# Layer 1 (windowed attention) of a four-layer megakernel, redone: centred weights, paired value products, norm copies on POOL, softmax in parts, source order on four engines

## The chip, the cores and the metric

The kernel runs on one core of one Trainium2 chip. The metric is the device time of one launch in microseconds (us), as the median of the runs shown. Everything is float32.

## The reference

Four residual layers are applied to an image batch x of 8 x 56 x 56 x 192 (NHWC). Each is `x = x + layer(group_norm(x))`, with a group norm of 32 groups of 6 channels. The layers are a Toeplitz token mixer, a shifted-window attention, a depthwise convolution with four exponential scans, and a 7x7 depthwise convolution with an MLP. The change touches the second, which is cut here to what matters:

```python
mu = jnp.mean(x, axis=-1, keepdims=True)              # over the 192 channels
var = jnp.var(x, axis=-1, keepdims=True)
x = (x - mu) * jax.lax.rsqrt(var + EPS) * gamma + beta
sx = jnp.roll(x, shift=(-3, -3), axis=(1, 2))
win = <7x7 windows of sx>                              # 64 windows of 49 tokens per image
q, k, v = (win @ w_qkv + b_qkv)                        # 6 heads of 32
attn = softmax(q * hd**-0.5 @ k.T + rel_bias + mask)
out = (attn @ v) @ w_proj + b_proj                     # windows back to the image, roll back
```

## The kernel before, in words

The launch runs layer 0, layer 1, layer 2 and layer 3 one after the other, each over all 8 images, with the images in DRAM between them. Channels lie on partitions: 64 channels of three blocks j = 0, 1, 2, and the upper and the lower half of an image on partitions 0 to 63 and 64 to 127 (s = 0, 1).

Layer 1 works on one image in four groups g. A group is one row of eight 7x7 windows in each half, so 392 tokens (TT) per half. A group's work is cut into parts, each a Python closure that issues its instructions when it is called:

- **N**: one step of the generator `layer1_norm` for the next image. It copies the image with the group norm's scale and shift into window order in `xr` (L703, five ACT activations per group), gets the mean over channels with a matmul of ones (L707) and subtracts it on DVE (L709), squares on ACT (L711), gets the variance with a second matmul (L715), and, once per image, takes root and reciprocal (L727, L728) and multiplies (L689, L691).
- **Q** (four per group): `project` in `layer1_scores`, matmuls of q or k for 96 of 192 channels (L748) and their evictions on ACT and DVE (L754 to L758).
- **V** (two per group): `values`, for each window and each half of the channels a product with 64 tokens as the stationary operand and 96 columns of weights as the moving one (L767), evicted on ACT and DVE (L775, L777).
- **E** (two per group, one per half s): `weights`. 48 small products of q and k into the PSUM tile S (L788), then bias and mask added on DVE (L795), the maximum (L797), its subtraction on POOL (L798), exp on ACT (L799), the sum and its reciprocal on DVE (L801, L802), and the multiplication on POOL (L803).
- **T** (six per group): `turn`, four transposes of the attention weights on PE (L823) into the `et_ps` tile, and a copy on ACT or DVE.
- **P** (two): `mix`, 48 small products of the weights with v (L838), and two copies that put windows back into image rows (L849, L851).
- **R** (three): `project` in `layer1_mix`, the output projection (L857) and its addition to the image on DVE (L864).

PSUM has three banks under the tag `mm`, taken in turn by Q, V, P, R and the norm (two each for Q, V and P), two for the transposes and three for S. While a group is mixed (T, P, R), the next one is projected and scored (Q, V, E), and the next image is normed (N), in an order that is written out by hand and holds for PE alone; what the other engines do, and when, is ordered by the planner from its own costs:

```python
plan = "T T Q N T T Q T P N T Q N Q P E N V E N V R R R".split()
st.enter_context(tc.manual_schedule(engines={mybir.EngineType.PE}))
```

The SP queue loads the images (`layer1_load`, three buffers), loads bias and mask for each half group (`bm`, two buffers) and stores the results. `build_bias_mask` prepares bias and mask during layer 0. The bn_stats for the group norm of layer 2 (L154) follow each group.

Of the kernel before, what the change touches and what calls it, by code (L numbers as in the profile page):

```python
# [10 lines left out]
F32 = mybir.dt.float32  # L11
# [8 lines left out]
HC = 96  # L20
TT = 392
# [8 lines left out]
HEADS, HD, WN = 6, 32, 49  # L30

# [56 lines left out]
def kernel(ctx: ExitStack, tc: tile.TileContext, a: dict, out: bass.AP):  # L88
# [215 lines left out]
    def build_bias_mask(psum, pool, masks):  # L304
# [31 lines left out]
        def add(g):  # L336
            bm = pool.tile([128, 3, 4, 2, WN], F32, name="bmt", bufs=1)
            for h in range(HEADS):
                nc.vector.tensor_tensor(
                    bm[:, h % 3, :, h // 3, :], mks[g], bt[:, h:h + 1, :].to_broadcast([128, 4, WN]), ALU.add  # L340
                )
            nc.gpsimd.dma_start(bmask[g], bm.rearrange("p a b c d -> p (a b c d)"))
# [277 lines left out]
    def layer1_weights(pool, psum):  # L620
# [29 lines left out]
        wg = pool.tile([128, 3, 3 * C], F32, name="wg", bufs=1)  # L650
        for j in range(3):
            nc.vector.tensor_scalar(wg[:, j], w_qkv[:, j], vec("g1", j), None, ALU.mult)
        nc.vector.tensor_scalar(wg[:, :, 0:C], wg[:, :, 0:C], HD ** -0.5, None, ALU.mult)
        return wg, bq, w_proj, bpr
# [19 lines left out]

    def layer1_norm(b, x, pool, psum, consts, first=False):

        ones2, ones32, sel = consts[4:]

        xr = pool.tile([128, 3 * NH + 16], F32, name="xr")
        nc.gpsimd.memset(xr[:, 3 * NH:], 0.0)
        xw = xr[:, 0:3 * NH].rearrange("p (j n) -> p j n", j=3)
        rs = pool.tile([128, TT], F32, name="rs1")

        def scaled(g):
            gs = bass.ts(g, TT)
            bp = psum.tile([128, 512], F32, name="rstd", tag="mm", bufs=3)[:, 0:TT]
            nc.tensor.matmul(bp, sel[32 * g:32 * g + 32], rs[32 * g:32 * g + 32], start=True, stop=True)  # L689
            xs = xw[:, :, gs]  # L690
            nc.vector.tensor_tensor(xs, xs, bp.unsqueeze(1).to_broadcast([128, 3, TT]), ALU.mult)  # L691

        yield xr
        sc, sh = scsh1[:, 0, b:b + 1], scsh1[:, 1, b:b + 1]
        for g in range(4):
            gs = bass.ts(g, TT)
            windows = xw[:, :, gs].rearrange("p c (w i j) -> p c w i j", i=7, j=7)
            xg = x[:, :, 7 * g:7 * g + 7]
            for dst, src in (
                *((windows[:, j, 0:7], xg[:, j, :, 3:52].rearrange("p i (w j) -> p w i j", j=7)) for j in range(3)),  # L700
                (windows[:, :, 7, :, 0:4], xg[:, :, :, 52:56]), (windows[:, :, 7, :, 4:7], xg[:, :, :, 0:3]),
            ):
                nc.scalar.activation(dst, src, AF.Identity, bias=sh, scale=sc)  # L703
            yield
            mp = psum.tile([128, 512], F32, name="mean", tag="mm", bufs=3)[:, 0:TT]
            for j in range(3):
                nc.tensor.matmul(mp, ones2, xw[:, j, gs], start=(j == 0), stop=(j == 2))  # L707
            xs = xw[:, :, gs]
            nc.vector.tensor_tensor(xs, xs, mp.unsqueeze(1).to_broadcast([128, 3, TT]), ALU.subtract)  # L709
            sq = pool.tile([128, 3, TT], F32, name="sq")  # L710
            nc.scalar.activation(sq, xs, AF.Square)  # L711
            yield
            vp = psum.tile([128, 512], F32, name="vps", tag="mm", bufs=3)[32 * g:32 * g + 32, 0:TT]
            for j in range(3):
                nc.tensor.matmul(vp, ones32, sq[:, j], start=(j == 0), stop=(j == 2))  # L715
            if not first:
                nc.vector.tensor_copy(rs[32 * g:32 * g + 32], vp)
                continue
            rg = rs[32 * g:32 * g + 32]
            nc.scalar.activation(rg, vp, AF.Sqrt, bias=eps5[32 * g:32 * g + 32])  # L720
            nc.vector.reciprocal(rg, rg)
            yield
            scaled(g)
            yield
        if first:
            return
        nc.scalar.activation(rs, rs, AF.Sqrt, bias=eps5)  # L727
        nc.vector.reciprocal(rs, rs)  # L728
        for g in range(4):
            yield  # L730
            scaled(g)

    def layer1_scores(g, xr, pool, psum, S, es, consts):
# [3 lines left out]
        xw = xr[:, 0:3 * NH].rearrange("p (j n) -> p j n", j=3)  # L737
        gs = bass.ts(g, TT)
        qk = [pool.tile([HC, 2, 2, TT], F32, name=f"qk{s}", bufs=1) for s in range(2)]

        v = [pool.tile([128, 8, HC], F32, name=f"v{s}") for s in range(2)]

        def project(which, m):
            ps = [psum.tile([128, 512], F32, name="qk_ps", tag="mm", bufs=3)[0:HC, 0:TT] for s in range(2)]
            c0 = which * C + m * HC
            for j in range(3):
                for s in range(2):
                    nc.tensor.matmul(  # L748
                        ps[s], wg[64 * s:64 * s + 64, j, c0:c0 + HC], xw[64 * s:64 * s + 64, j, gs],
                        start=(j == 0), stop=(j == 2),  # L750
                    )
# [8 lines left out]
        def values(w4):  # L760
            ps = [psum.tile([128, 512], F32, name="v_ps", tag="mm", bufs=3)[:, 0:4 * HC] for s in range(2)]
            for w in range(4):
                for j in range(3):
                    for p in range(2):
                        for s in range(2):
                            t0 = j * NH + g * TT + WN * (w4 + w)
                            nc.tensor.matmul(  # L767
                                ps[s][64 * p:64 * p + 64, HC * w:HC * w + HC], xr[64 * s:64 * s + 64, t0:t0 + 64],
                                wg[64 * s:64 * s + 64, j, 2 * C + HC * p:2 * C + HC * p + HC],
                                start=(j == 0), stop=(j == 2),  # L770
                            )
            for s in range(2):
                dst = v[s][:, w4:w4 + 4].rearrange("p w c -> p (w c)")
# [5 lines left out]
        def weights(s):  # L779
            bm = pool.tile([128, 24, WN], F32, name="bm")  # L780
            nc.sync.dma_start(bm.rearrange("p a b -> p (a b)"), bmask[4 * s + g])


            for w in range(8):
                cs = slice(WN * w, WN * w + WN)
                for h in range(HEADS):
                    p0 = 32 * (h % 3)
                    nc.tensor.matmul(  # L788
                        S[64 * (w % 2):64 * (w % 2) + WN, 8 * (h % 3) + w // 2 * 2 + h // 3, 0:WN],
                        qk[s][p0:p0 + 32, 0, h // 3, cs], qk[s][p0:p0 + 32, 1, h // 3, cs],  # L790
                        start=True, stop=True,
                    )
            e = es[g % 2][s]
            ev = e[:, :, 0:WN]
# [3 lines left out]
            nc.gpsimd.tensor_tensor(ev, ev, mx.unsqueeze(2).to_broadcast([128, 24, WN]), ALU.subtract)  # L798
            nc.scalar.activation(ev, ev, AF.Exp)  # L799
            sm = pool.tile([128, 24], F32, name="sm")  # L800
# [4 lines left out]
        return v, [  # L805
            [lambda which=which, m=m: project(which, m) for which in range(2) for m in range(2)],
            [lambda w4=w4: values(w4) for w4 in (0, 4)], [lambda s=s: weights(s) for s in range(2)],
        ]

    def layer1_mix(g, x, v, pool, psum, es, consts):  # L810
# [21 lines left out]
        def mix(s):  # L832
            et, o = ets[s], oa[s]
            po = [psum.tile([128, 512], F32, name="po", tag="mm", bufs=3)[0:HC, 0:TT] for _ in range(2)]
            for w in range(8):
                for r in range(3):
                    for hh in range(2):
                        nc.tensor.matmul(  # L838
                            po[hh][32 * r:32 * r + 32, WN * w:WN * w + WN],
                            v[s][64 * hh:64 * hh + WN, w, HD * r:HD * r + HD],  # L840
                            et[64 * hh:64 * hh + WN, 4 * r + w // 2, 64 * (w % 2):64 * (w % 2) + WN],
                            start=True, stop=True,
                        )

            for hh in range(2):
                dst = o[:, hh].rearrange("p (i w j) -> p w i j", i=7, j=7)
                src = po[hh].rearrange("p (w i j) -> p w i j", i=7, j=7)
                if hh == 0:
# [4 lines left out]
        def project(j):  # L853
            ps = psum.tile([128, 512], F32, name="pr", tag="mm", bufs=3)[:, 0:TT]
            for m in range(2):
                for s in range(2):
                    nc.tensor.matmul(  # L857
                        ps[64 * s:64 * s + 64], w_proj[:, m, 64 * j:64 * j + 64], oa[s][:, m],
                        start=(m == 0), stop=(m == 1),
# [6 lines left out]
        return [  # L866
            [lambda s=s, i=i: turn(s, i) for s in range(2) for i in range(3)],
            [lambda s=s: mix(s) for s in range(2)], [lambda j=j: project(j) for j in range(3)],
        ]
# [447 lines left out]
    with ExitStack() as st:  # L1317
        pool = st.enter_context(tc.tile_pool(reuse_waits="tile", name="l1", bufs=2))
        psum = st.enter_context(tc.tile_pool(reuse_waits="tile", name="l1p", bufs=1, space=PSUM))
        consts = layer1_weights(pool, psum)  # L1320

# [5 lines left out]
        for s in range(2):  # L1327
            nc.gpsimd.memset(ones2[64 * s:64 * s + 64, 64 * s:64 * s + 64], 1.0 / C)
            nc.gpsimd.memset(ones32[64 * s:64 * s + 64, 16 * s:16 * s + 16], 1.0 / C)
        nc.gpsimd.dma_start(sel, a["sel"])  # L1330
# [6 lines left out]
        consts = (*consts, ones2, ones32, sel)  # L1337
# [3 lines left out]
        for _ in range(4):  # L1341
            next(own)
        if nimg > 1:
            x.append(layer1_load(1, xpool))
        values, (Q, V, E) = layer1_scores(0, xr[0], pool, psum, S, es, consts)
# [263 lines left out]
```

## Time and profile before

| what | value |
|---|---|
| median of three runs | 5983.35 us (5983.24 to 5999.2) |
| the profiled execution | 5980.23 us |
| its span | 5978.3 us |
| busy share of PE, DVE, ACT, POOL over the span | 89%, 56%, 37%, 22% |
| layer 1, from the last store of layer 0 to the last addition (L864) | 2055.7 to 3366.3 us |
| busy in images 1 to 6 of it (952.5 us): PE, DVE, ACT, POOL | 805.33, 493.99, 328.67, 209.77 us |
| granted TensorE clock there | 0.92 |

The span runs from the first to the last instruction of the profiled execution; the launch's own time is 1.9 us longer. Busy time is the union of an engine's instructions, and PE's is modelled, since matmuls are pipelined. A float32 matmul shows up as two PE instructions (passes), each with its weight load (PEld). A wait named "issue" is time in which an engine waited for nothing that the profile shows.

### The profile page before, as it was taken

The numbers are of one execution on the slowest core, as the hardware profiler recorded it, in microseconds if no ns is written. First come the engines' busy times: TensorE is split into PE (matmuls) and PEld (weight loads), VectorE is DVE, ScalarE is ACT, GpSimd is POOL, SyncE is SP. The second block draws the span as 40 slices with busy tenths as digits, with TensorE's granted clock in tenths as the row PEclk, the third lists the DMA queues.
The fourth block names the chain that finished last, engine by engine and source line by source line (L and its number), as shares of the span: only waits on it lengthen the run. The fifth ranks groups of instructions, "written<-read, shape, count | busy, mean of one in ns | idle before, by whom it ended". The sixth has DMA issues, their size and how long they took to land. (4 is left out here: it accounts for less than half of the span.)

```text
span 5978.3 us, 124904 instructions
## 1 busy us (share of the span) xinstructions
PE 5305.3 (89%) x54932; PEld 3442.4 (58%) x54932; DVE 3367.4 (56%) x4698; ACT 2225.5 (37%) x2993; POOL 1299.5 (22%) x862
## 2 busy tenths in 40 slices
PE   6899989999998888888888798999788799799999
PEld 4668756666665545455555475777444399444444
DVE  6777765555555455554555586888877401533331
ACT  2344443333333333333332102455466600333333
POOL 2100024444444212222222102333201100200100
PEclk8999989999999999899998899999899899899999
DMA  6899886666666502222211576677577598321210
GB/s 176 208 229 219 193 249 246 242 259 255 256 252 252 156 26 67 67 66 59 67 51 55 136 256 224 229 233 235 162 214 209 181 337 292 126 76 59 90 41 25
DMA packets 703411, 1012.59 MB, mean 169 GB/s; under 512 B 484888, under 2 KB 621636, under 8 KB 676100
## 3 DMA queue, kind: packets, MB, share of 16 engines
q1 hardware_dynamic: 688464, 940.25, 50.4%
q0 software_dynamic: 8256, 39.67, 2.0%
q10 hardware_dynamic: 6148, 24.68, 1.3%
q8 instruction: 432, 7.08, 0.5%
q14 instruction: 111, 0.91, 0.0%
HBM read 675.89 MB, written 345.08 MB: 171 GB/s over the span
## 5 line engine op out<-in xcount | busy, mean ns | idle before, releaser
L383 PE MATMUL qv<-w_qv_sb,xn 64*112 64x288 f32 x5376 | 710.0, 420 | 41.5 <-DVE act L389 38.0
L421 POOL COPY lc<-lt 128x896 f32<-128x896 f32 (+1 forms) x320 | 550.5, 1744 | 646.2 <-PE op L429 544.0
L383 PEld LDWEIGHTS qv<-w_qv_sb,xn 64*112 64x112 f32 x5376 | 535.5, 181 | 211.0 <-DVE act L389 53.9
L390 ACT ACTIVATE act<-act 112x576 f32<-112x576 f32 x448 | 300.0, 682 | 441.9 <-DVE act L389 405.0
L429 PE MATMUL op<-rc,lc 128*56 128x56 f32 x9216 | 339.7, 220 | 101.6 <-POOL lc L421 67.0
L429 PEld LDWEIGHTS op<-rc,lc 128*56 128x56 f32 x9216 | 307.4, 135 | 177.0 <-POOL lc L421 94.1
L1227 PE MATMUL ph<-y,w_sb 64*128 64x392 f32 x2304 | 398.3, 498 | 6.4 <-ACT hid L1231 6.4
L1238 PE MATMUL po<-hid,w_sb 128*64 128x392 f32 x2304 | 386.3, 494 | 0.0
L1245 DVE TENSOR_TENSOR x<-x,z 128x392 f32<-128x392 f32 x96 | 70.8, 737 | 522.4 <-ACT z L1243 522.4
L389 DVE TENSOR_TENSOR act<-qv,b_qv 112x576 f32<-112x576 f32 x448 | 320.8, 752 | 76.3 <-PE qv L383 75.9
L421 ACT COPY rc<-rt 128x896 f32<-128x896 f32 (+1 forms) x160 | 256.4, 1607 | 248.6 <-PE op L429 232.9
L954 PE MATMUL cv<-zc,wt 128*128 128x224 f32 x1536 | 313.2, 356 | 24.3 <-DMA zc<-pd 23.9
L954 PEld LDWEIGHTS cv<-zc,wt 128*128 128x128 f32 x1536 | 290.5, 190 | 67.9 <-issue 51.9
L1227 PEld LDWEIGHTS ph<-y,w_sb 64*128 64x128 f32 x2304 | 220.6, 189 | 176.0 <-issue 25.9
L441 PE MATMUL pj<-xn,w_p_sb 64*128 64x392 f32 x1536 | 309.0, 510 | 11.5 <-issue 7.3
L1128 PE MATMUL cps<-zc,wt 128*128 128x224 f32 x1536 | 299.2, 356 | 17.1 <-DMA zc<-zd 16.9
L798 POOL TENSOR_TENSOR e<-e,mx 128x1176 f32<-128x1176 f32 x64 | 139.7, 2183 | 789.4 <-DVE mx L797 622.5
L1128 PEld LDWEIGHTS cps<-zc,wt 128*128 128x128 f32 x1536 | 289.2, 189 | 27.2 <-issue 19.7
L748 PE MATMUL qk_ps<-xr,wg 64*96 64x392 f32 x1536 | 298.9, 511 | 1.7 <-DVE xr L691 1.5
L462 PE MATMUL y<-pp,w_o_sb 128*64 128x392 f32 x1536 | 288.3, 505 | 6.7 <-DVE x L470 3.9
L1238 PEld LDWEIGHTS po<-hid,w_sb 128*64 128x64 f32 x2304 | 162.7, 137 | 213.8 <-issue 213.8
L455 DVE TENSOR_TENSOR pp<-pp,ot 128x784 f32<-128x784 f32 x128 | 124.2, 970 | 286.1 <-ACT pp L446 276.3
(228 smaller groups left out, 9138.7 us busy)
## 6 DMA issues: line engine op xcount, KB each, us to landing
lt<-left SPq DMA_DIRECT2D x72, 1792.0 KB
rt<-right SPq DMA_DIRECT2D x72, 1792.0 KB
left<-qv SPq DMA_DIRECT2D x224, 252.0 KB
right<-qv SPq DMA_DIRECT2D x448, 126.0 KB
wt<-in_band_dram SPq DMA_DIRECT2D x23, 2048.0 KB
wt<-in_band_dram SPq DMA_DIRECT2D x11, 4096.0 KB
zc<-pd SPq DMA_DIRECT2D x187, 232.0 KB
pd<-pt SPq DMA_DIRECT2D x7, 5568.0 KB
```

Source lines behind the costliest of these rows:

```text
L383: nc.tensor.matmul(ps[s][:, which, 0:D1 // 2], xn[64 * s:64 * s + 64, j, bass.ts(i, 2 * W)], w_qv[64 * s:64 * s + 64, j, which, ns], start ...
L389: nc.vector.tensor_tensor(act, ps[s][:, :, 0:D1 // 2], b_qv[:, :, ns], ALU.add)
L390: nc.scalar.activation(act, act, AF.Silu)
L421: copy(c[:, 0:nu], raw.rearrange("p (w u d) -> p u d w", u=nu, d=64 // nu)[:, :, d0:d0 + 8])
L429: nc.tensor.matmul(op[64 * u:64 * u + W, i, :], lc[:, u, i], rc[:, u, i], start=True, stop=True)
L441: nc.tensor.matmul(ps[0:M, s, 0:TT], w_p[64 * s:64 * s + 64, j, d0:d0 + M], xn[64 * s:64 * s + 64, j, ts], start=(j == 0), stop=(j == 2),)
L462: nc.tensor.matmul(y[64 * s:64 * s + 64], w_o[0:M, c, 64 * j:64 * j + 64], pp[0:M, s], start=(c == gated[0][0]), stop=(c == gated[-1][0]),)
L748: nc.tensor.matmul(ps[s], wg[64 * s:64 * s + 64, j, c0:c0 + HC], xw[64 * s:64 * s + 64, j, gs], start=(j == 0), stop=(j == 2),)
L954: nc.tensor.matmul(dst, wt[:, c4 + i, 128 * q:128 * q + 128], zc[:, :, c4 + i, q:q + NPAIR], start=(q == 0), stop=(q == 1),)
L1128: nc.tensor.matmul(dst.rearrange("p (b n) -> p b n", n=NPAIR), wt[:, c4 + i, q * OP:(q + 1) * OP], zc[:, :, c4 + i, q:q + NPAIR], start=(q ...
L1227: nc.tensor.matmul(ps[:, s, 0:TT], w0[64 * s:64 * s + 64, j, m * 128:(m + 1) * 128], y[64 * s:64 * s + 64, j, ts], start=(j == 0), stop=(j ...
L1238: nc.tensor.matmul(ps[64 * s:64 * s + 64], w1[:, m, 64 * j:64 * j + 64], hid[:, m, s], start=(m == 0), stop=(m == 5),)
```

## The change

All of it lies in layer 1 and in the order of `bmask`, which it reads.

1. The mean over channels is taken out of the weights once (`layer1_weights` subtracts from each weight the mean over its 192 inputs), so the tokens aren't centred any more. The variance becomes the mean of squares less the square of the mean, from one bank that takes both sums of two groups in four strips of 32 partitions.
2. `xr` is laid out so that two windows stand in one block of 113 columns, 64 apart with zeros between. A value product takes 128 columns of it (two windows) as the stationary operand, with all 192 columns of weights as the moving one. The transposes, mixes, scores and bias follow that order, and the reordering from windows to image rows goes from the copies after the mix to the moving operand of the output projection.
3. The copies into `xr` are done by POOL (`tensor_scalar`), eight per group; for the first image by ACT, DVE and POOL in turn.
4. The softmax of a half group is cut into E (scores to the subtraction), X (exp) and Y (sum, reciprocal, multiplication); X and Y are called in the next group's plan. The bn_stats of a group (G) are called in the next group's plan too.
5. The plan is new, with more and smaller norm steps, and it orders ACT, DVE and POOL as well as PE. The first image's norm is finished ahead of the plan, and an image's norm is finished ahead of the last group.

```diff
-        wg = pool.tile([128, 3, 3 * C], F32, name="wg", bufs=1)
         for j in range(3):
-            nc.vector.tensor_scalar(wg[:, j], w_qkv[:, j], vec("g1", j), None, ALU.mult)
-        nc.vector.tensor_scalar(wg[:, :, 0:C], wg[:, :, 0:C], HD ** -0.5, None, ALU.mult)
-        return wg, bq, w_proj, bpr
+            nc.vector.tensor_scalar(w_qkv[:, j], w_qkv[:, j], vec("g1", j), None, ALU.mult)
+        nc.vector.tensor_scalar(w_qkv[:, :, 0:C], w_qkv[:, :, 0:C], HD ** -0.5, None, ALU.mult)
+        for which in range(3):
+            cs = slice(which * C, (which + 1) * C)
+            ps = psum.tile([128, 512], F32, name="wmean", tag="mm", bufs=3)[:, 0:C]
+            for j in range(3):
+                nc.tensor.matmul(ps, ones2, w_qkv[:, j, cs], start=(j == 0), stop=(j == 2))
+            nc.vector.tensor_tensor(
+                w_qkv[:, :, cs], w_qkv[:, :, cs], ps.unsqueeze(1).to_broadcast([128, 3, C]), ALU.subtract
+            )
+        return w_qkv, bq, w_proj, bpr
...
+            for n, (dst, src) in enumerate(copies):
+                if first and n % 3 == 1:
+                    nc.scalar.activation(dst, src, AF.Identity, bias=sh, scale=sc)
+                else:
+                    eng = nc.vector if first and n % 3 == 2 else nc.gpsimd
+                    eng.tensor_scalar(dst, src, sc, sh, ALU.mult, ALU.add)
+                if n % 2:
+                    yield
...
+        def finish(rows):
+            nc.vector.tensor_scalar(rs[rows], rs[rows], 0.0, 1e-5, ALU.max, ALU.add)
+            nc.scalar.activation(rs[rows], rs[rows], AF.Sqrt)
+            nc.vector.reciprocal(rs[rows], rs[rows])
...
+            ps = psum.tile([128, 512], F32, name="stat", tag="mm", bufs=3)
+            for j in range(3):
+                for k in range(n):
+                    nc.tensor.matmul(
+                        in_pairs(ps[32 * k:32 * k + 32, 0:TT]), ones32, in_slots(xr, (4 * j + g0 + k) * GW),
+                        start=(j == 0), stop=(j == 2),
+                    )
+                    nc.tensor.matmul(
+                        ps[64 + 32 * k:96 + 32 * k, 0:TT].rearrange("p (z n) -> p z n", z=2), ones32, sqs[k][:, :, j],
+                        start=(j == 0), stop=(j == 2),
+                    )
...
+            nc.vector.tensor_tensor(rs[to], ps[rows, 0:TT], msq[rows], ALU.subtract)
...
-        def values(w4):
-            ps = [psum.tile([128, 512], F32, name="v_ps", tag="mm", bufs=3)[:, 0:4 * HC] for s in range(2)]
-            for w in range(4):
+        def values(k0):
+            ps = [psum.tile([128, 512], F32, name="v_ps", tag="mm", bufs=3)[:, 0:2 * C] for s in range(2)]
+            for k in range(2):
                 for j in range(3):
-                    for p in range(2):
-                        for s in range(2):
-                            t0 = j * NH + g * TT + WN * (w4 + w)
-                            nc.tensor.matmul(
-                                ps[s][64 * p:64 * p + 64, HC * w:HC * w + HC], xr[64 * s:64 * s + 64, t0:t0 + 64],
-                                wg[64 * s:64 * s + 64, j, 2 * C + HC * p:2 * C + HC * p + HC],
-                                start=(j == 0), stop=(j == 2),
-                            )
+                    for s in range(2):
+                        t0 = (4 * j + g) * GW + PW * (k0 + k)
+                        nc.tensor.matmul(
+                            ps[s][:, C * k:C * k + C], xr[64 * s:64 * s + 64, t0:t0 + 128],
+                            wg[64 * s:64 * s + 64, j, 2 * C:3 * C], start=(j == 0), stop=(j == 2),
+                        )
...
+        def exponents(s):
+            ev = es[g % 2][s][:, :, 0:WN]
             nc.scalar.activation(ev, ev, AF.Exp)
+
+        def shares(s):
+            ev = es[g % 2][s][:, :, 0:WN]
             sm = pool.tile([128, 24], F32, name="sm")
             nc.vector.tensor_reduce(sm, ev, AX.X, ALU.add)
             nc.vector.reciprocal(sm, sm)
             nc.gpsimd.tensor_tensor(ev, ev, sm.unsqueeze(2).to_broadcast([128, 24, WN]), ALU.mult)
...
-        plan = "T T Q N T T Q T P N T Q N Q P E N V E N V R R R".split()
-        st.enter_context(tc.manual_schedule(engines={mybir.EngineType.PE}))
+        plan = "X Q Y V X G Q N Y T T T N V N T N N Q G P N T T G N Q N P N N E N R R N E N R".split()
+        st.enter_context(tc.manual_schedule(
+            engines={mybir.EngineType.PE, mybir.EngineType.Activation, mybir.EngineType.DVE, mybir.EngineType.Pool}
+        ))
...
+                if g == 3:
+                    run(steps)
```

## The prediction

> **What bounds the kernel now.** I began with the page: the change touches layer 1 alone, so I looked for its slices (14 to 22 of 40, 149.5 us each).
>
> ```profile
> PE   6899989999998888888888798999788799799999
> DVE  6777765555555455554555586888877401533331
> ACT  2344443333333333333332102455466600333333
> POOL 2100024444444212222222102333201100200100
> PEclk8999989999999999899998899999899899899999
> ```
>
> PE stands at 8 or 9, nothing else above 5. By the windows view, layer 1 is a prologue of 66 us, image 0 in 171.1 us, images 1 to 6 in 952.5 us (158.75 each) and image 7 in 120.6 us. One image, its four groups apart (columns: stretch, its us, then busy us of PE, PEld, DVE, ACT, POOL, granted clock, DMA share, GB/s):
>
> ```profile
> 2293.20:2337.00 43.80, 35.98 (x696) 20.75 (x694) 20.34 (x30) 15.61 (x26) 8.25 (x4) 0.88 0.62 140
> 2337.00:2379.50 42.50, 37.82 (x701) 22.66 (x699) 24.14 (x33) 16.85 (x25) 8.70 (x5) 0.92 0.10 31
> 2379.50:2416.70 37.20, 30.74 (x672) 18.78 (x669) 21.09 (x29) 12.96 (x23) 9.24 (x6) 0.87 0.11 35
> 2416.70:2451.20 34.50, 28.94 (x678) 18.27 (x676) 16.61 (x26) 10.01 (x18) 8.77 (x5) 0.95 0.11 37
> sum 158.00, PE 133.48 PEld 80.46 DVE 82.18 ACT 55.43 POOL 34.96; mean PE 33.37 PEld 20.12 DVE 20.55 ACT 13.86 POOL 8.74
> ```
>
> PE is the bound, with 24.5 us of idling in 158; DVE has half its time free. The waits of PE from 2170 to 3340 us (some 29 groups) say what it idles on:
>
> ```profile
> PE S L788 <- issue: 57.8, 26, 6.1
> PE v_ps L767 <- issue: 44.5, 27, 5.2
> PE pr L857 <- ACT v L775: 30.6, 24, 2.8
> PE po L838 <- ACT qk L754: 10.9, 7, 1.6
> PE po L838 <- ACT qk L756: 10.1, 20, 0.8
> ```
>
> "Issue" is the largest: 102 us, 3.5 per group, only where runs of small matmuls stand (scores S, values v). The third line is the ring of three `mm` banks: an exp on ACT waits for POOL, the copy of v waits behind the exp, and the output projection waits for v's bank.
>
> Timeline rows at full clock price the parts (start, busy us):
>
> ```profile
> 2641.86 1.26 PE L788 MATMUL S<-qk 32*49 32x49 f32 x96
> 2643.16 2.16 PE L715 MATMUL vps<-sq,ones 128*32 128x392 f32 x6
> 2645.25 2.21 PE L767 MATMUL v_ps<-wg,xr 64*64 64x96 f32 x96
> 2651.46 1.54 PE L857 MATMUL pr<-oa,w_proj_sb 96*64 96x392 f32 x8 [1.21 <-ACT v L775]
> 2652.93 1.09 PE L823 MATMUL et_ps<-ident,e 128*128 128x128 f32 x8
> 2653.95 2.28 PE L748 MATMUL qk_ps<-xr,wg 64*96 64x392 f32 x12
> ```
>
> From start to start, in such rows: transposes 0.51 for four, one Q 2.15, S 1.19, mix 1.15, v 2.15, output projection 1.47, mean 2.15, variance 2.10, rstd 0.85. Per image (four groups): T 12.2, Q 34.4, S 9.5, P 9.2, V 17.2, R 17.6, mean and variance 17.0, rstd 3.4: **120.5 us**. The measured 158.75 is that plus 24.5 of idling plus some 13.7 for half-clock stretches. Both losses are local to the S/V runs.
>
> [...] in 3.4 us stretches the granted clock is 1.00 or 0.50, and it fell to 0.50 after a stretch with 2.10 us of 3.40 busy. [...] 432 instruction packets, 7.08 MB, 16.4 KB each; so an issue wait is a late fetch, and the worst ones fall where the DMA share is near 1. [...] here only two column tiles are seen (row L857: 8 passes of 392 columns in 1.47 us, 0.18 each, against 0.36 for the untiled variance). [...] a POOL tensor_scalar of 1568 elements has a median of 1.65 us here, 1.05 ns each.
>
> **The change, part by part, per image.**
> *Mean into the weights.* Mean matmuls (8.6 us of PE) and four 1.38 us subtractions on DVE go. Sums and squares now go to four column strips of one bank: 24 passes of 392 columns for two groups. At four-way overlap 24 x 0.36 / 4 = 2.15 us per pair; at the two-way that is shown, 4.3. I take 2.15: 4.3 per image for 17.0, **PE -12.7** (-8.4 at the other end). Once, centring the weights: 18 passes of 192 columns and three 0.7 us subtractions, about 5 us, beside the first image's norm; 0 to +5.
> *Values.* 192 instructions of 64x96 become 48 of 64x192 with 128 stationary columns. A Q pass of 392 columns costs 0.179, so one of 192 about 0.094: 4.5 us per group for 4.3, **PE +0.8**. What it buys is instructions: load and matmul counted, a group falls from about 1370 to 1070, in the S/V run from 768 to 384 plus 48 for R. By rate fetch waits would fall from 14 to about 8 per image; since S and P now have long matmuls between them I take **5**, bounds 2 and 14.
> *Norm copies.* 20 ACT activations per image (12 us) go; 32 POOL tensor_scalar come, 4 x 1176 elements, at 1.05 ns (above) to 2.15 ns (strided L421 copy: 1.93 us for 896) plus 0.1 each: 8 to 13 us, and pads 0.7 (the 128x720 memset). POOL then has 8.7 + 6.5 = 15 us in a group of over 30: hidden. On ACT the squares come in halves and the squared means are new, about +2 in all, net -10; hidden.
> *Softmax in parts.* exp, sum and shares move to the next group. No ACT copy waits behind an exp that waits for POOL: the pr waits (49.7 us with those on DVE, 1.7 per group) go. Late next: Q and V now stand back to back on the three-bank ring. I count seven handovers per group (V after Q, Q after V, the next Q after V, the two P after Q, and the third transpose of each half on its two banks), each 0.1 + an eviction of 0.46 to 0.69 + 0.1 less what lies between, about 0.7: 4.9, **20 per image**. Behind exp on ACT stand Q's evictions; its subtraction was issued a whole R earlier, so it doesn't wait.
> *Norm's finish* in source order: 0.35 + table 1.28 + sqrt 0.6 + reciprocal 2.6 ahead of the first rstd matmul, of which three transposes hide 1.5: **3** per image. DVE evictions are queued behind that reciprocal.
> *Reordering of the mixed heads.* It moves from the eviction copy to the moving operand of R (runs of 7). Runs of 28 in the cv matmul cost nothing visible (356 ns for 224 columns); bounds 0 and +7 per image, I take 0.
> *bmask layout, bn_stats one group later, queues:* same counts. The SP queue keeps its loads and stores; bias loads still have two buffers and stand behind image transfers of some 15 us, inside a 30 us group. Zero, at most +5 per image if the cover goes.
> *Half clock:* [...] I take **3** for 13.7, bounds 1 and 14.
>
> Image: 120.5 - 12.7 + 0.8 = 108.6, + 20 + 3 + 5 + 3 = **140 for 158.75**. Times six: -112. Image 0: 171 to 145 (140 and one group-norm chain of 5): -26. Image 7 has no next norm: three groups of about 32, and a last group of 20 where it took 10.9, because exp and shares have nothing beside them: 117 for 120.6, -4. Prologue: a chain shorter by mean and subtraction, but all four groups' norm inside it: 0, +-8. Sum **-142**. The profiled execution took 5980.2 (span 5978.3); the median of three is 3.1 above, so 5983.35 - 142 = 5841, said as **5840**.
>
> **Rivals.**
> *Losses stay.* If handovers, fetches and half clock together cost what they do now (38 to 40), an image is 148.5: 6 x -10.25, image 0 -17, image 7 about 0: 5905. For it: seven handovers where T and Q now alternate. Against: the fetch waits sit exactly in the run that shrinks.
> *Losses nearly go.* Handovers at half, fetch and clock about 4: 128 per image, 6 x -31, -38, -10: 5750. For it: every engine but PE has over a third of its time free.
> *Slower: head-of-line blocking.* DVE no longer picks what is ready. A softmax pass of 1.38 us ahead of an eviction makes a handover 2.1 instead of 0.7. With 11 us for the rest, an image equals 158.75 when seven handovers cost 9.8 us per group, 1.4 each: that is from every second handover on. At seven in ten it is 0.7 + 0.98 = 1.68, an image 167, and 6 x 8, image 0 +1, image 7 +18 is +67: 6050. For it: the L775 wait is this very thing. Against: in the plan the passes mostly stand ahead of evictions with PE work in between (E, then R).
> *Not what it says:* POOL as the bound of the norm groups needs 2.2 us per copy against 0.17 to 0.53 priced; I give it no chance of its own.
>
> **Numbers.** About 0.3% (18 us) is what a measurement can tell from no change. Main case 0.50 (5775 to 5890), losses stay 0.20 (up to 5965), losses nearly go 0.16, no change 0.05, slower 0.09. Faster 0.86, same 0.05, slower 0.09. The range 5745 to 5930 takes the main case, most of its two neighbours, and leaves 2 in 10 out.
>
> **What would show it.** Stat matmuls of a pair near 2.2 us (right) or 4.3; v near 2.2 us per half; the windows of images 1 to 6 near 140, the last group near 20; S and V issue waits under 1.5 us per group; PEclk of layer 1 above 0.96; POOL under 16 us per group. Wrong would be: PE waiting on DVE evictions with more than 7 us per group, issue waits as before, or POOL's copies beyond 1 us each.

## The result and the profile after

| what | before | after |
|---|---|---|
| median | 5990.34 us of 4 runs (5983.24 to 5999.2) | 5918.16 us of 4 runs (5903.67 to 5924.04) |
| profiled execution, its span | 5980.23, 5978.3 us | 5919.44, 5917.7 us |
| images 1 to 6 of layer 1, each | 158.8 us | 150.8 us |
| of it PE busy, idle | 134.2, 24.5 us | 132.0, 18.8 us |
| of it at half clock | 26.2 us | 43.3 us |
| groups 0, 1, 2, 3 of an image, mean | 43.1, 44.8, 37.0, 33.9 us | 42.0, 30.2, 45.6, 33.0 us |

The changed kernel takes 0.9875 of the time before (95% interval 0.985 to 0.99): 72 us less, where 142 were forecast. Groups here end with the last addition to the image on DVE. Of the 60.6 us by which the profiled spans differ, images 1 to 6 give 47.8, image 7 gives 9.0 (111.6 for 120.6) and everything up to the end of image 0 gives 4.0; the rest is 0.2 longer.

The slices of the page, in the same order as those of before:

```profile
PE   6889989999999888888898798999788799799999
DVE  6777765555555445555555686888787410533331
ACT  2334444333333333333333103555476500333333
POOL 2100025444444323333332103333110100200100
PEclk8899989999999988888888899999899899899999
```

PE is still at 8 in layer 1, and its clock line went the wrong way: 9s became 8s. The windows view of one image (stretch, its us, busy us of PE, PEld, DVE, ACT, POOL, granted clock, DMA share, GB/s) shows that this is no even loss:

```profile
2440.20:2482.80 42.60, 34.67 (x558) 19.79 (x556) 17.81 (x28) 12.85 (x22) 18.53 (x23) 0.82 0.64 150
2482.80:2512.90 30.10, 28.76 (x554) 17.37 (x552) 17.89 (x28) 12.86 (x22) 15.54 (x20) 1.00 0.14 42
2512.90:2559.80 46.90, 39.82 (x546) 23.91 (x542) 25.78 (x37) 12.75 (x19) 7.77 (x5) 0.78 0.07 20
2559.80:2592.60 32.80, 30.10 (x522) 17.81 (x522) 17.02 (x26) 9.75 (x16) 8.73 (x5) 0.83 0.13 41
```

Group 1 is what the change can do: clock 1.00, 30.1 us. Group 0 holds nearly the same PE instructions (558 for 554) and takes 12.5 us more. The waits of PE from 2182 to 3224 us (line, releaser: us in total, times, longest):

```profile
PE S L838 <- issue: 57.3, 17, 8.5
PE et_ps L879 <- ACT et L884: 18.8, 28, 2.0
PE po L893 <- ACT qk L810: 17.0, 49, 0.4
PE rstd L743 <- DVE rs L739: 10.6, 7, 1.5
PE v_ps L820 <- ACT qk L808: 10.4, 28, 0.9
PE qk_ps L802 <- DVE xr L748: 7.6, 14, 0.8
```

The issue wait of V is gone, and so is the output projection's on the copy of v. The issue wait of S is what it was (57.3 for 57.8), in fewer and longer pieces. The trace shows what it waits for. In images 1 to 6 it holds up S 16 times, and each time a 16 KB packet of the instruction queue (q8) landed 1.2 to 1.8 us before S went on. PE and its weight loads used 254 instructions per such packet. In the same images of before, S and V waited on "issue" for more than 1 us 37 times, each time with such a packet 1.2 to 1.6 us earlier, one per 256 instructions. So I read these waits as late fetches of instructions. Now the PE timeline of group 3 (start, busy us; in brackets the idling before it):

```profile
2577.55 1.08 PE L893 MATMUL po<-et,v 49*32 49x49 f32 x94 [0.36 <-ACT qk L810]
2578.56 1.20 PE L838 MATMUL S<-qk 32*49 32x49 f32 x78
2581.33 0.43 PE L838 MATMUL S<-qk 32*49 32x49 f32 x18 [1.57 <-issue]
2581.69 5.48 PE L912 MATMUL pr<-oa,w_proj_sb 96*64 96x392 f32 x16
2587.10 1.93 PE L838 MATMUL S<-qk 32*49 32x49 f32 x96
2588.95 2.88 PE L912 MATMUL pr<-oa,w_proj_sb 96*64 96x392 f32 x8
```

The same stretch of group 1 has no wait:

```profile
2502.71 1.37 PE L838 MATMUL S<-qk 32*49 32x49 f32 x96
2504.01 3.10 PE L912 MATMUL pr<-oa,w_proj_sb 96*64 96x392 f32 x16
2507.03 1.37 PE L838 MATMUL S<-qk 32*49 32x49 f32 x96
2508.33 0.52 PE L760 MATMUL stat<-xr,ones 128*32 128x392 f32 x1
2508.34 0.52 PE L764 MATMUL stat<-sq,ones 128*32 128x392 f32 x1
2508.34 0.52 PE L760 MATMUL stat<-xr,ones 128*32 128x392 f32 x1
2508.35 0.52 PE L764 MATMUL stat<-sq,ones 128*32 128x392 f32 x1
```

A fetch that is 1.57 us late (its packet ran from 2579.03 to 2580.09, S went on at 2581.33) is followed by an output projection of 5.48 us where it takes 3.10. The granted clock in this trace is 1.00 or 0.50, and its 179 changes lie within 0.02 us of a grid of 3.413 us, as the 183 of before do. The windows view at about these steps shows why:

```profile
2578.30:2581.70 3.40, 1.83 (x133) 1.58 (x120) 0.56 (x1) 0.48 (x1) 0.00 (x0) 1.00 0.02 5
2581.70:2585.10 3.40, 3.40 (x18) 1.31 (x14) 3.14 (x3) 0.00 (x0) 0.24 (x1) 0.51 0.25 48
2585.10:2588.50 3.40, 3.40 (x90) 1.77 (x92) 1.03 (x4) 1.20 (x1) 1.95 (x1) 0.50 0.33 134
2588.50:2591.90 3.40, 3.40 (x41) 1.25 (x35) 2.74 (x3) 0.00 (x0) 0.00 (x0) 0.50 0.18 32
2591.90:2595.40 3.50, 3.50 (x12) 1.68 (x13) 2.32 (x5) 0.00 (x0) 3.33 (x4) 0.50 0.82 238
2595.40:2598.80 3.40, 2.99 (x28) 2.17 (x26) 0.05 (x1) 1.42 (x3) 2.67 (x3) 1.00 0.98 201
```

The clock drops after one window with 1.83 us of work; four follow with PE busy throughout and the clock at half, until one of nothing but Q passes. Three windows of R and S, busy throughout by the profile (3.40 of 3.40 us), did not bring the full clock back, so PE's busy time in a window doesn't settle when it returns. The kind of matmul doesn't settle it either: seven other half-clock windows of this trace that R alone filled did bring the full clock back, as the first of these does:

```profile
2551.03:2554.45 3.42, 3.42 (x14) 2.00 (x10) 1.09 (x3) 0.72 (x1) 2.18 (x1) 0.50 0.48 164
2554.45:2557.86 3.41, 3.41 (x109) 1.86 (x108) 2.26 (x4) 0.49 (x1) 0.00 (x0) 1.00 0.00 0
```

What brings the clock back stays open.

**Theory.** Each image has three losses, in groups 0, 2 and 3, and each goes with a stretch at half clock (granted clock 0.82, 0.78 and 0.83 above, 1.00 in group 1). In groups 0 and 3 it is a late fetch in the first scores, because the plan's "P N N E" puts two runs of 49-column matmuls back to back: 384 instructions with the weight loads, the last 380 of which take 2.31 us in group 1 (2501.70 to 2504.01). At that rate the 254 of a packet last 1.5 us (an estimate), while from the start of the late packet in group 3 to S's going on 2.3 us passed. In group 0 the fetch also stands among the transfers of the image being loaded:

```profile
2461.00:2471.00 10.00, 3.41 (x150) 2.45 (x136) 1.65 (x2) 1.77 (x3) 0.95 (x3) 0.74 0.99 207
```

DMA share 0.99, and PE busy 3.41 us of 10; the packet that S waits for starts at 2466.18, 3.8 us into the wait. Image 6 loads no further image: its wait was 1.6 us for 6.6 to 8.5 in images 1 to 5, its group 0 took 36.4 us for 42.5 to 43.6. In group 2 it is the norm's root (from image 3 on, a fetch wait of 1.4 to 1.9 us comes on top). The ACT timeline:

```profile
2520.30 1.28 ACT L738 ACT_TABLE_LOAD   x1
2521.59 0.53 ACT L738 ACTIVATE rs<-rs 128x392 f32<-128x392 f32 x1
2522.03 0.57 ACT L884 COPY et<-et_ps 128x512 f32<-128x512 f32 x1
```

The table load and the root stand ahead of a transpose's copy, so PE waits 1.96 us for a bank of `et_ps`, then 1.51 us for the reciprocal:

```profile
2522.65 0.66 PE L879 MATMUL et_ps<-ident,e 128*128 128x128 f32 x4 [1.96 <-ACT et L884]
2524.81 1.67 PE L743 MATMUL rstd<-rs,sel 32*128 32x392 f32 x2 [1.51 <-DVE rs L739]
```

The clock falls at 2523.7, and a second time at 2534.0, after a window in which PE was busy for 3.10 of 3.41 us, mostly with the rstd products of 32 rows and transposes.

**Rivals.** The handovers between PE and the evictions; POOL's copies; the paired value products; the source order itself.

### The profile page after: what moved, and what is told of

Same layout as the page of the kernel before. It is cut to its first block, busy times and chain, and to the rows that moved or that the text cites. A ratio compares the mean times of both kernels' runs of the same rounds, so it can differ in the third digit from the quotient of the medians.

```text
span 5917.7 us, 116084 instructions
## 1 busy us (share of the span) xinstructions
PE 5286.4 (89%) x50342; PEld 3409.5 (58%) x50342; DVE 3346.7 (57%) x4710; ACT 2170.9 (37%) x2911; POOL 1411.5 (24%) x1106
## 5 line engine op out<-in xcount | busy, mean ns | idle before, releaser
L386 PE MATMUL qv<-w_qv_sb,xn 64*112 64x288 f32 x5376 | 710.4, 422 | 39.8 <-DVE act L392 36.5
L802 PE MATMUL qk_ps<-xr,w_qkv_sb 64*96 64x392 f32 x1536 | 349.5, 549 | 10.9 <-DVE xr L748 10.9
L1028 POOL TENSOR_TENSOR rows<-rows,loc 128x896 f32<-128x896 f32 x96 | 220.0, 2292 | 255.7 <-ACT rows L1024 205.9
```

What stands on the lines that cost most here:

```text
L386: nc.tensor.matmul(ps[s][:, which, 0:D1 // 2], xn[64 * s:64 * s + 64, j, bass.ts(i, 2 * W)], w_qv[64 * s:64 * s + 64, j, which, ns], start ...
L802: nc.tensor.matmul(in_pairs(ps[s]), wg[64 * s:64 * s + 64, j, c0:c0 + HC], in_slots(xr[64 * s:64 * s + 64], (4 * j + g) * GW), start=(j == ...
```

## The experiments

Ratios are to the kernel before, timed on the same chip; its medians there were 5985.34, 5989.67 and 5986.06 us. Kernels of different tables are compared by their ratios, one hundredth being 60 us. "Issue" and "half clock" are us per image.

### Order of SyncE, place of V, and a later root

*sp_order* adds SyncE to the engines in source order:

```diff
-    engines={... mybir.EngineType.DVE, mybir.EngineType.Pool}
+    engines={... mybir.EngineType.DVE, mybir.EngineType.Pool, mybir.EngineType.SP}
```

*v_after_s* and *v_before_s* move the first V of the plan to the scores, behind or ahead of the first run:

```diff
-plan = "X Q Y V X G Q N Y T T T N V N T N N Q G P N T T G N Q N P N N E N R R N E N R"
+plan = "X Q Y X G Q N Y T T T N V N T N N Q G P N T T G N Q N P N N E V N R R N E N R"   # v_after_s
+plan = "X Q Y X G Q N Y T T T N V N T N N Q G P N T T G N Q N P N V N E N R R N E N R"   # v_before_s
```

*rstd_later* gives the root three more steps:

```diff
         finish(slice(0, 128))
+        for _ in range(3):
+            yield
         for g in range(4):
```

> SP joins the engines in source order, so the load of an image leaves one group after the store of another instead of together with it. Theory (instruction fetch is held up by the image transfers, and the half clock follows from it): the wait of 6 to 8 us in the scores of group 0 goes, with the half-clock stretch behind it; group 0 of images 1 to 6 from 43 to 33-36 us, in all -45 to -65 us against the changed kernel (some 5855 to 5875). Rival (the wait in group 0 has nothing to do with transfers, but with the number of instructions in the run): within 10 us of the changed kernel, group 0 still 43.

> The first value product V of a group moves from the start of the plan to behind the first scores E, ahead of the two R. Theory [...]: the half-clock stretches of groups 0 and 3 shrink from 13.7 to about 7 us, 3 to 4 us less per stretch, -30 to -60 us in all. Rival 1 (the clock comes back after a fixed time whatever runs): within 10 us. Rival 2 (more instructions in the run of scores mean more fetch waits): +10 to +60 us.

> The first V moves to between the second mix P and the first scores E, which otherwise stand back to back with 384 instructions in 2.3 us. Theory (a fetch is late by what a run of small matmuls leaves it too little time for): the 1.6 us wait of group 3 goes and with it its half-clock stretch, group 3 from 33 to about 28 us; in group 0 the wait falls by about 2 us and the clock still drops; -30 to -60 us in all. Rival (the waits sit at the block's boundary wherever it falls and only move): within 10 us.

> Three empty norm steps stand between the root and reciprocal of the norm and the first multiplication, so that the rstd matmuls come about 8 us later in group 2. Theory: PE no longer waits for the reciprocal (1.5 us and 1.1 us on the multiplications), and with it one of the half-clock stretches of group 2 goes; group 2 from 45-47 to about 40 us, -25 to -50 us in all. Rival (the transposes' wait behind the root on ACT, 2 us, is enough to drop the clock): -10 to -15 us.

| kernel | median us | ratio (95%) | an image | groups | issue, half clock |
|---|---|---|---|---|---|
| sp_order | 5874.61 | 0.9812 (0.979 to 0.9833) | 143.4 | 35.1, 30.1, 45.3, 32.8 | 5.2, 32.4 |
| v_after_s | 5886.41 | 0.9834 (0.9817 to 0.9851) | 143.7 | 39.4, 32.3, 42.0, 30.0 | 8.9, 25.6 |
| v_before_s | 5841.74 | 0.9752 (0.9736 to 0.9769) | 136.6 | 37.8, 30.8, 38.7, 29.3 | 4.3, 13.7 |
| rstd_later | 5897.88 | 0.985 (0.9827 to 0.9873) | 147.3 | 41.2, 30.2, 42.4, 33.5 | 10.5, 33.5 |

SyncE's order changes group 0 alone (42.0 to 35.1), and by the ratios takes 38 us off, for 45 to 65 expected: the planner had put the load of image b+2, written in group 2, next to the store of image b. S in group 0 now waits 1.7 to 2.3 us for its fetch, in images 1 to 5 too.

V between P and the scores leaves the same work in another order and takes 74 us off the total, more than was expected. Groups 2 and 3 have no late fetch any more, group 0 keeps 4.4 to 5.7 us of it in images 1 to 5, and half-clock time falls from 43.3 to 13.7 us. Group 2 gains most (45.6 to 38.7), in images 1 and 2 too, where it had no fetch wait; the waits for the root are still there, and why they now cost less half-clock time no run shows.

V behind the first scores takes two fifths of the half-clock time away but leaves the issue waits (8.9 for 9.4). In group 0 the stretch at half clock gets shorter (9.6 us for 14.3). In group 3 PE now waits 0.6 to 1.1 us in images 1 to 5 and 1.7 us in image 6, and the clock doesn't fall.

The later root moves group 2 by 3.2 us, and the total by 15 us, less than the measurement can tell: the intervals overlap. That is the rival's size. The wait for the reciprocal is gone, but the 1.96 us for the bank stay, and the next transposes wait 1.8 to 3.3 us for POOL's multiplication.

### The other parts of the change

*v_four* takes the four small value products per pair again, *act_copies* gives the copies to ACT, *pe_only* leaves source order to PE alone, and *heat* adds three long matmuls to an unread bank behind the first scores:

```diff
-for k in range(2):
-    for j in range(3):
-        for s in range(2):
+for k, p, j, z, s in np.ndindex(2, 2, 3, 2, 2):        # v_four: 64x64 tiles, 96 columns each
...
-if first and n % 3 == 1:
+if not first or n % 3 == 1:                             # act_copies
...
-engines={PE, Activation, DVE, Pool}
+engines={PE}                                            # pe_only
...
+if s == 0:                                              # heat
+    hot = psum.tile([128, 512], F32, name="hot", tag="mm", bufs=3)[:, 0:TT]
+    for j in range(3):
+        nc.tensor.matmul(in_pairs(hot), ident, in_slots(xr, (4 * j + g) * GW), start=(j == 0), stop=(j == 2))
```

> The value products go back to four tiles of 64x64 with 96 columns, 192 instructions per group instead of 48; layout, plan and everything else stay as changed. Theory (pairing saves instructions, not PE time, and where V now stands, between Q and T, a fetch has time): +0 to +30 us against the changed kernel, a half of V near 2.2 us as before. Rival (the pairing of the value products is where the gain came from): +50 to +110 us, near the kernel before.

> The copies into window order are done by ACT again (eight activations per group of the norm), not by POOL. Theory (both engines have room, PE sets the time): within 15 us of the changed kernel, or up to +25 where evictions stand behind a copy. Rival (ACT, in source order, delays the evictions that PE waits for): +40 us or more, with PE waiting on ACT qk and ACT v in groups 0 and 1.

> Source order for PE alone, as before; ACT, DVE and POOL are ordered by the planner, all else as changed. Theory (the order took away the waits behind exp, 1.7 us per group, and PE's own waits): +20 to +60 us. Rival (what the softmax's new place in the plan does is done by PE's order alone): within 15 us.

> Six passes of 128x128 with 392 columns are added behind the first scores of each group, 2.15 us at full clock, 8.6 us per image, into a bank that nobody reads; nothing is left out. Theory (dense passes bring the clock back, R and E don't): the half-clock stretches of groups 0 and 3 get shorter by about half, which pays for the added work: -20 to +25 us in all. Rival (the clock comes back after a fixed time): +60 to +95 us.

| kernel | median us | ratio (95%) | an image | groups | issue, half clock |
|---|---|---|---|---|---|
| v_four | 5899.91 | 0.9846 (0.9819 to 0.9874) | 146.3 | 40.1, 32.7, 42.5, 31.0 | 8.7, 30.7 |
| act_copies | 5923.26 | 0.9882 (0.9859 to 0.9904) | 148.5 | 40.8, 31.2, 43.9, 32.6 | 9.9, 34.7 |
| pe_only | 6038.01 | 1.0074 (1.0056 to 1.0093) | 163.3 | 40.3, 40.1, 45.1, 37.8 | 9.0, 46.2 |
| heat | 5923.38 | 0.9886 (0.9863 to 0.9908) | 147.8 | 37.0, 33.5, 46.2, 31.2 | 5.9, 22.8 |

The paired products give nothing of their own (v_four's interval overlaps the changed kernel's 0.985 to 0.99, from below), and the copies cost the same on either engine: neither is where the gain came from. Source order is worth some 120 us, for 20 to 60 expected: without it the change is 0.7% slower than the kernel before. What the centred weights with the statistics in strips give by themselves was not run apart. The waits of *pe_only*:

```profile
PE v_ps L820 <- ACT qk L808: 72.2, 24, 6.9
PE S L838 <- issue: 50.6, 18, 7.7
```

The planner lets Q's eviction on ACT come late, 3 us on average, and V stands behind it. *heat* is inconclusive: it cut the half-clock time by 20 us an image, but its own matmuls (6 passes of 392 columns in a group, some 2.2 us at the 0.36 that such a pass took in the variance) took back what that gave, and it shifted the stream of instructions as well.

### All three together, the phase of the fetches, and source order alone

*together* is v_before_s with SyncE in source order, four more steps ahead of the root and two behind it. *shift* and *v_before_s_shift* put 128 short PE instructions, 32 matmuls, ahead of layer 1's plan, half of the 254 or so that PE used per packet. They took 13.8 us where 2 had been expected.

```diff
+pad = psum.tile([128, 512], F32, name="pad", tag="mm", bufs=3)
+for _ in range(32):
+    nc.tensor.matmul(pad[:, 0:1], ident, ident[:, 0:1], start=True, stop=True)
```

*before_source_order* is the kernel before with `engines={PE, Activation, DVE, Pool}`.

> The changed kernel with three edits at once: the value half between P and the first scores (as in v_before_s), SyncE's queue in source order too (as in sp_order), and the finish of the square root given four more steps before its copies and two more before the scaling. Theory (three separate losses: the first scores' late instruction fetch, the fetch held up behind the image transfers of group 0, the table load and the late root in group 2): group 0 falls to about 31 to 34 us, group 2 to about 35, an image of layer 1 to 126 to 129 us, the total to 5775 to 5795 us, 50 to 65 us below v_before_s's 5842. Rival (v_before_s has already taken away what the others repair, since each of them only started the same stretch at half clock): within 20 us of v_before_s.

> The changed kernel with 32 matmuls of one column ahead of everything, 128 or fewer TensorE instructions that take about 2 us in all: nothing else differs but where in the instruction stream the boundaries of fetched blocks fall. Theory (the place of a boundary decides which group's first scores wait): the pattern of groups 42.0, 30.2, 45.6, 33.0 us changes, with the waits of 1.5 to 6.6 us in other groups than 0 and 3, and the total moves by 20 to 60 us either way. Rival (the length of the run of tiny score matmuls alone decides, wherever the boundaries fall): the same groups within 1 us and a total within 10 us of the changed kernel.

> v_before_s with the same 32 matmuls of one column in front. Theory (the value half between the two runs of tiny score matmuls gives the fetch time, wherever the boundaries fall): within 15 us of v_before_s, 5830 to 5857 us. Rival (v_before_s was lucky in where its boundaries fell): back towards the changed kernel, 5880 us or more.

> The kernel before, with its own plan, softmax in one piece and uncentred weights, but with ScalarE, VectorE and GpSimd held to source order as in the change. Theory (source order pays only with the softmax written in parts: in one piece its exponentials and multiplications stand ahead of evictions on ScalarE and VectorE): slower than before by 100 us or more. Rival (source order alone is what pays; pe_only showed it to be worth 120 us in the changed kernel): faster than before by 50 us or more.

| kernel | median us | ratio (95%) | an image | groups | issue, half clock |
|---|---|---|---|---|---|
| together | 5764.77 | 0.9628 (0.9608 to 0.9647) | 126.4 | 32.2, 30.7, 34.1, 29.3 | 0.1, 2.8 |
| shift | 5861.59 | 0.9793 (0.9771 to 0.9814) | 139.9 | 35.1, 34.8, 41.9, 28.0 | 5.6, 25.6 |
| v_before_s_shift | 5842.36 | 0.9755 (0.9737 to 0.9774) | 136.0 | 36.1, 30.8, 39.8, 29.3 | 2.7, 13.1 |
| before_source_order | 6138.67 | 1.0252 (1.0232 to 1.0272) | 179.4 | 51.5, 51.3, 40.3, 36.4 | 12.3, 50.6 |

*shift* moves layer 1 by 128 instructions in the stream and leaves the plan as it is, and some 50 us go, the 13.8 us of the pad already paid. Its windows view of one image:

```profile
2448.70:2485.70 37.00, 31.12 (x548) 18.10 (x548) 17.54 (x28) 12.83 (x22) 18.59 (x23) 0.91 0.74 173
2485.70:2520.50 34.80, 31.58 (x556) 18.38 (x554) 18.11 (x29) 12.85 (x22) 15.56 (x20) 0.90 0.12 37
2520.50:2564.00 43.50, 38.14 (x546) 22.19 (x542) 25.53 (x36) 12.75 (x19) 7.71 (x5) 0.80 0.07 23
2564.00:2592.10 28.10, 26.97 (x530) 16.66 (x528) 17.00 (x27) 9.76 (x16) 8.81 (x5) 1.00 0.14 46
```

The wait has left groups 2 and 3; group 3 now has clock 1.00 and 28.0 us for 33.0. It has come into group 1, where waits of 1.6 to 2.2 us cost 4.6 (34.8 for 30.2). So a fetch wait of some 1.6 us costs about 5 us, in the very same instructions. In *v_before_s* the same shift leaves the total as it was (5842.36 for 5841.74) and an image within 1 us (136.0 for 136.6): with value products ahead of the scores this shift doesn't matter.

*together* comes by the ratios to 74 us below v_before_s and 148 below the changed kernel: 10 us better than the edge of what was expected. One image of it, by the windows view, and its largest waits of PE from 2182 to 3100 us:

```profile
2391.70:2423.00 31.30, 28.60 (x548) 17.26 (x548) 17.55 (x28) 12.58 (x22) 17.78 (x23) 1.00 0.58 157
2423.00:2453.90 30.90, 29.46 (x556) 17.63 (x554) 17.88 (x29) 12.69 (x22) 16.25 (x21) 1.00 0.50 119
2453.90:2487.80 33.90, 31.35 (x546) 18.14 (x542) 25.19 (x37) 13.01 (x20) 7.75 (x5) 1.00 0.10 28
2487.80:2517.20 29.40, 26.73 (x528) 17.33 (x528) 16.95 (x27) 9.37 (x16) 8.80 (x5) 1.00 0.04 15
```

```profile
PE et_ps L883 <- POOL e L862: 20.0, 16, 1.5
PE po L897 <- ACT qk L814: 19.1, 51, 0.5
PE et_ps L883 <- ACT et L888: 6.9, 29, 0.2
```

The clock is full in all four groups of this image (2.8 us an image are at half clock on average, most of them in group 0), S waits for no fetch, and what is late next is POOL's multiplication ahead of the first transposes. This is the fastest kernel of the study. How its last 74 us divide between SyncE's order and the root was not run apart; the groups they act in, 0 and 2, gained 5.6 and 4.6 us.

Source order in the kernel before costs 153 us. Its waits of PE:

```profile
PE S L788 <- issue: 58.6, 23, 7.5
PE pr L857 <- ACT v L775: 57.1, 21, 4.8
PE rstd L689 <- DVE rs L728: 34.2, 7, 6.7
```

The wait on the copy of v nearly doubled (57.1 for 30.6): with the softmax in one piece its exp stands ahead of that copy for good. Neither paid without the other here: source order alone costs 153 us, and the whole change without source order is slower than the kernel before. The softmax in parts with nothing else of the change was not run.

## Why the prediction was right and wrong

*What held.* The direction and the range. The stat matmuls of a pair take 2.1 us (24 passes from 2508.33 to 2510.5, 0.09 us each where the variance before took 0.36): four strips do overlap. A V half takes 2.22 us in the stall-free group. POOL is busy 12.6 us a group on average (303.55 over 24 groups; 18.5 in group 0) and never the bound. Its copies take 514 ns for 196 elements and 417 for 63, so the price by element with 0.1 us for each copy (the smallest POOL memsets of before take 98 ns) was the wrong form at this size: an image's 32 copies took 15.3 us for 8 to 13 said, hidden all the same. The last group takes 18.6 us for 20 forecast. R's new runs of 7 cost nothing by themselves (16 passes in 3.10 us, where 8 took 1.54 before). No eviction on DVE cost PE more than 2 us at a time (its longest wait on DVE from 2182 to 3224 us was 1.7): the blocking that the slower rival feared came only with the softmax in one piece (*before_source_order*), and there behind ACT's exp more than on DVE.

*The sum.* Full-clock work can be read from *together*, which has the same layer-1 instructions: 117.5 us busy less half of its 2.8 at half clock, 116.1 (an estimate). The changed kernel's 150.8 is then:

| term | predicted | measured |
|---|---|---|
| PE work at full clock | 108.6 | 116.1 |
| handovers and the norm's finish | 20 + 3 | 9.4 (18.8 idle less 9.4 issue) |
| late fetches | 5 | 9.4 |
| half clock | 3 | 15.9 (132.0 busy less 116.1) |
| image | 140 | 150.8 |

*The step that failed is the half clock:* "I take 3 for 13.7, bounds 1 and 14", an estimate of mine whose ground no trace showed. The time at half clock rose, from 26.2 to 43.3 us, and the 15.9 us by which it stretches PE's work are above the upper bound. I counted idle windows, as if each cost itself alone. But after the late fetch ahead of R in group 3 the clock stayed down for four windows. Nor does PE's busy time in a window settle whether the clock falls: on the grid of 3.41 us, PE was busy for 3.10 of 3.41 us in a window of the changed kernel that was followed by half clock (2530.55 to 2533.96), and for 1.58 of 3.41 in one of the kernel before that was not (3041.80 to 3045.21). And the term rests on an earlier step that misread the plan: "since S and P now have long matmuls between them I take 5". The second P and the first E have only norm steps between them, back to back as in the plan before, while the value products, which shrank, were moved away. *v_before_s* puts long matmuls there and takes back 29.6 us of half-clock time and 5.1 us of fetch wait per image. Over six images the 12.9 us by which the term was too small come to 77 us; the profiled executions missed the forecast by 81 (60.6 for 142). Of the other terms, image 0 and the prologue add 22 us, and the rest nearly cancel that.

*Two sizes that cancel in part.* I priced a handover at 0.7 us of idling, with an estimated 0.1 on each side of an eviction (in before PE starts 0.05 us after the end of the ACT instruction that releases it, in the median); PE idles 0.2 to 0.4 at most of them (17.0 us in 49 waits of P, 10.4 in 28 of V). Work is 7.5 us above the sum of starts, and waiting 13.6 below. Part of that may be one thing counted on two sides: an R pass is shown for 0.52 us while the next starts after 0.17 on average (2504.01 to 2506.58), so ahead of a wait the end of a pass counts as busy. No run here divides it.

*Image 0* was to give 26 us and the prologue none; both together gave 4.0. From the end of the bias matmuls to the first matmul of the norm, 8.5 us now pass, with the 18 passes of the centring in 5.41 of them and two waits, where the norm had started at once. The second wait is for a copy of the norm that stood on DVE behind the centring's subtractions. So the centring is on the path, above its bound of 5. The first image then has the same stalls in groups 0, 2 and 3 as the others.

*By the rivals,* "losses stay" (5905) was the nearest number: fetches, handovers and clock cost 34.7 us an image, for 38 to 40 said. But they are other losses than before.

## What to carry to other kernels

Price a PE wait by what runs behind it, not by its length: where output projections and scores follow, 1.6 us of waiting cost 5 here. Put longer matmuls between runs of tiny ones: the value products took all fetch waits out of groups 2 and 3 and 14.2 us off an image; a pad of short instructions ahead of the stage tells in one run whether a stall hangs on the place of instructions in the stream. Giving all engines the order of the source, the DMA queue too, paid here only together with a source that had been cut so that no exp stands ahead of an eviction for long.

## What was not expected of the hardware

- In the changed kernel the clock did not return under three 3.4 us windows that PE filled with output projections and scores (2581.7 to 2591.9); it did after one that Q filled (2591.9 to 2595.4), and after seven that output projections alone filled (the first from 2551.03).
- It fell after a window with PE busy for 3.10 of 3.41 us, and in the kernel before it stayed full after one with 1.58.
- 128 instructions of one column ahead of layer 1 moved the total by some 50 us, and fetch waits moved from groups 2 and 3 to group 1 with it.
- In the changed kernel a late instruction fetch held S up for 1.4 to 2.1 us by itself, and for 6.6 to 8.5 us while an image was being loaded; its packet landed 1.2 to 1.8 us before S went on.
- POOL's tensor_scalar on 128 partitions took 417 ns for 63 elements and 514 for 196; the line through both meets zero elements at some 370 ns (an estimate).
